# A decoder layer on one core: maxima units in twos between whole blocks, and every block in a PSUM tile of its own

## The chip, the core and the metric

The kernel runs on one core of a Trainium2 chip. Four engines matter here. TensorE (PE) multiplies matrices and writes to PSUM; a second row, PEld, is its weight loading. VectorE (DVE), ScalarE (ACT) and GpSimd (POOL) do the elementwise work, and SyncE (SP) issues most DMAs. Each engine runs its own instructions strictly in the written order and waits at semaphores that the framework sets. The metric is device microseconds (us) of one execution; the median of three runs is 805.79 us (805.64 to 805.87).

## The reference, cut to what matters

A decoder layer in float32: causal self-attention, causal attention of the result over a context, and a feed-forward part with a gated expert, each with its residual; B = 4 batch entries, S = 512 positions, D = 512, 16 heads of 32.

```python
def attention(q, k, v):                      # 4 x 16 heads of 512 x 32
    scores = einsum('bhqd,bhkd->bhqk', q, k) * SCALE
    scores = where(causal, scores, -inf)     # -10000 in the cross-attention
    return einsum('bhqk,bhkd->bhqd', softmax(scores), v)

x = x + attention(x_ln @ wq.T + bq, x_ln @ wk.T + bk, x_ln @ wv.T + bv) @ wo.T + bo
x = x + attention(layernorm(x), ctx, ctx)
f = layernorm(x)
x = x + relu(f @ W_up.T) @ W_down.T + sum_softmax_top2(f @ W_gate.T) * (f @ W_expert)
```

## The kernel before, in words

Everything of one batch entry lies in SBUF. Projections are made in **blocks**: four matmuls of 128x128 weights and 512 columns that add into one PSUM bank (`project`, L229; `project_t`, L241). In float32 each matmul is two records in the trace, so a block is eight records. A head has 32 rows, so the scores of the four heads of a group `g` run side by side in four row groups of the array, as 32x128 matmuls.

An attention goes in two stages. **The maxima** (`with_maxima`, `Attention.maxima`): the row maxima of the scores, to be subtracted before the exponential. There are ten *units* `u0` to `u9`, each one or two pieces `(g, i)` of 512 columns in all, for four heads, in two PSUM tiles `sm` (two heads each; below "a" and "b"). Per unit PE makes the scores (L293), ACT copies each tile to SBUF (L304), POOL masks the diagonal (L312), and DVE takes the maxima (L324). When the last piece of a group is done, `split` cuts the negated maxima into three bfloat16 parts on DVE (L346 to L350), and `rows` turns them over with four PE transposes into a tile `mt` (L361), which DVE, or ACT in the later stage, copies to `mrow` (L367). **The attention itself** (`attend`): ten units again, `S0` to `S9`; `scores` makes the transposed scores (L405) and adds the maxima with a bfloat16 matmul over `mrow` (L416), ACT takes the exponential (L439), POOL masks (L447), and `values` multiplies with v (L482) two units later.

`with_maxima` weaves other blocks between its units, matmul by matmul, as evenly as their number allows: after each unit so many matmuls (`count`) of the blocks in `steps`. What these are differs. In the self-attention of entry 0 they are its own last query and key blocks and its value blocks; of entries 1 and 2 the feed-forward part of the entry before (gate, up, down); of entry 3 four expert blocks and two up blocks. In the cross-attentions they are the query and key blocks of the next entry (and expert blocks in entry 1), in entry 3 the gate and four down blocks. Behind each matmul one `job` is set down: a DVE reduction, the `split`, or a layernorm step of the next entry. A unit's jobs are set down in the gap after the *next* unit.

`ps` is a pool of four PSUM tiles of two banks, each 512 floats wide (`pair`). Blocks come in twos: a query and a key block share a tile, as do two value, up, down or expert blocks, and one instruction of ACT or DVE empties both (value: L685 on DVE; up: L790 on ACT; down: L843 on DVE; query and key are two ACT instructions, L645 and L648, after the second; expert: L867 on DVE, one for each). A new tile takes the one of the four that was released first in the written order. PE then waits until the last reader of the old content is through.

The order of all four engines is the written order (`manual_schedule`).

Of the kernel before, what the change touches and what calls it, by code (L numbers as in the profile page):

```python
# [18 lines left out]
P = 128  # L19
# [7 lines left out]
def decoder_layer(  # L27
# [37 lines left out]
    def pair(name):  # L65

        return ps.tile([P, 2, S], F32, tag="ps", name=name)


# [196 lines left out]
    class Attention:  # L266
# [84 lines left out]

        def rows(self, g, both=None, half=0):


            if both is None:
                tp = ps.tile([P, NT, P], BF16, tag="ps", name=f"mt_{self.name}_{g}")
            else:
                bank = both[:, 0, :].bitcast(BF16)
                tp = bank[:, half * S : (half + 1) * S].rearrange("p (i q) -> p i q", q=P)
            for i in range(NT):  # L360
                nc.tensor.transpose(tp[:, i, :], parts[g % 2][:, i, :], identb)  # L361
            self.mrow[g] = work.tile(
                [P, S], BF16, tag="mrow", name=f"mrow_{self.name}_{g}", bufs=4
            )

            def copy(engine=nc.vector.tensor_copy):
                engine(self.mrow[g], tp.rearrange("p i q -> p (i q)"))  # L367

            return [copy]
# [261 lines left out]
    def query_key(e):  # L631
        b, made = e.b, {}
        e.q_t = act.tile([P, NC, S], F32, tag="q_t", name=f"qT_{b}")
        e.k_t = act.tile([P, NC, S], F32, tag="k_t", name=f"kT_{b}")

        def query(f):
            made[f] = pair(f"pm_qk{b}_{f}")
            yield from project_t(made[f][:, 0, :], wq_sb, e.xn_t, f)

        def key(f):  # L640
            yield from project_t(made[f][:, 1, :], wk_sb, e.xn_t, f)
            out(f)

        def out(f):
            nc.scalar.activation(  # L645
                e.k_t[:, f, :], made[f][:, 1, :], AF.Identity, bias=bk_sb[:, f : f + 1]
            )
            nc.scalar.activation(  # L648
                e.q_t[:, f, :],
                made[f][:, 0, :],  # L650
                AF.Identity,
                bias=bqs_sb[:, f : f + 1],
                scale=SCALE,
            )

        def half(n):

            if n == 0:
                made[0] = pair(f"pm_qk{b}_0")
            rows = slice(n * S // 2, (n + 1) * S // 2)  # L660
            for c in range(NC):
                nc.tensor.matmul(
                    made[0][:, 0, rows],
                    lhsT=wq_sb[:, c, :P],
                    rhs=e.xn_t[:, c, rows],
                    start=(n == 0 and c == 0),
                    stop=(n == 1 and c == NC - 1),
                    skip_group_check=True,
                )

        steps = [(lambda f=f, w=w: w(f)) for f in range(NC) for w in (query, key)]
        if b == 0:
            steps[:1] = [lambda: half(0), lambda: half(1)]
        return steps

    def value(e):
        b, made = e.b, {}
        e.v = act.tile([P, NT, D], F32, tag="v", name=f"v_{b}")

        def one(t):  # L680
            if t % 2 == 0:
                made[0] = pair(f"pm_v{b}_{t}")
            yield from project(made[0][:, t % 2, :], e.xn_t, wv_sb, t)
            if t % 2 == 1:
                nc.vector.tensor_tensor(  # L685
                    e.v[:, t - 1 : t + 1, :],
                    made[0],
                    bv_sb.unsqueeze(1).to_broadcast([P, 2, D]),
                    ALU.add,
                )  # L690

        return [(lambda t=t: one(t)) for t in range(NT)]
# [85 lines left out]
    def ffn(e):  # L778
        b, f_t, made = e.b, e.f_t, {}

        def up(f):
            if f == 0:
                made["h"] = act.tile(
                    [P, NC, S], F32, tag="o_t" if b != B - 2 else "f_t", name=f"hT_{b}"
                )
            if f % 2 == 0:
                made["u"] = pair(f"pm_u{b}_{f}")
            yield from project_t(made["u"][:, f % 2, :], wup_sb, f_t, f)
            if f % 2 == 1:
                nc.scalar.activation(made["h"][:, f - 1 : f + 1, :], made["u"], AF.Relu)  # L790

        def share():

            made["g"] = pair(f"lg_{b}")
            part = made["g"][:, 0, :]
            for c in range(NC):
# [10 lines left out]
        def gate():  # L807
            lg = made["g"][:, 1, : NT * NE].rearrange("p (t e) -> p t e", e=NE)
            for t in range(NT):
# [24 lines left out]
        def down(t):  # L834
            if t % 2 == 0:
                made["d"] = pair(f"pm_d{b}_{t}")
            yield from project(made["d"][:, t % 2, :], made["h"], wdown_sb, t)
            if t == NT - 1 and b == B - 2:
                for n in range(2):
                    aside(f"d{b}_{n}", t - 1 + n, made["d"][:, n, :])  # L840
            elif t % 2 == 1:
                both = e.x[:, t - 1 : t + 1, :]
                nc.vector.tensor_tensor(both, made["d"], both, ALU.add)  # L843

        def expert(t):
            if b == B - 1 and t == NT - 1:
                yield from expert_parts(t)
                return
            last = b == B - 1 and t == NT - 2
            if t % 2 == 0:  # L850
                made["e"] = pair(f"pm_e{b}_{t}")
            yield from project(made["e"][:, t % 2, :], f_t, wexp_sb, t)
            for n in (0,) if last else (0, 1) if t % 2 == 1 else ():
                u = t - t % 2 + n
                weigh(u, made["e"][:, n, :], slice(0, D), nc.sync)

# [47 lines left out]

    def with_maxima(steps, a, first=0, norms=()):


        norms = list(norms)
        run(steps[:first])
        fill = matmuls(steps[first:])  # L910
        total = sum(1 if step.__name__ in ("share", "gate") else NC for step in steps[first:])

        units = []
        for g in range(0, NC, 2):
            units += [[(g, 1), (g + 1, 1)]]
            units += [u for k in (g, g + 1) for u in ([(k, 2), (k, 0)], [(k, NT - 1)])]

        lead = 2 if first else 0
        for _ in range(lead):
            next(fill)  # L920
        done, due, jobs, late = lead, float(lead), [], {3: NC - 1}
        todo = []
        for n, pieces in enumerate(units):
            new = a.maxima(pieces)
            if todo:
                todo.pop()(nc.gpsimd)
            if norms and n % 2 == 0:
                new.append(norms.pop(0))
            due += (total - lead) / len(units)

            count = round(due) - done
            for k in range(count):
                next(fill, None)
                done += 1
                if k == min(1, count - 1) and n in (5, 7):
                    jobs = a.rows((n - 5) // 2) + jobs
                if k == min(1, count - 1) and a.cross and n in (6, 8):
                    todo.append(a.masked(*a.masked_sums((n - 6) // 2)))
                if n == len(units) - 1 and k == count - (2 if count > 4 else 1):
                    if total >= 2 * len(units):  # L940
                        if a.cross:
                            a.rows(2)[0](nc.scalar.copy)
                    else:
                        late = {3: 2, 5: NC - 1}
                run(jobs[:1])
                jobs = jobs[1:]
            run(jobs)
            jobs = new
        for _ in fill:
            pass  # L950
        run(jobs)
        return late

    def attend(a, late):


        units = []
        for g in range(0, NC, 2):
            units += [[(g, 0)], [(g, 3), (g, 1)], [(g, 2), (g + 1, 2)]]
            units += [[(g + 1, 0)], [(g + 1, 3), (g + 1, 1)]]  # L960
        waiting, held, todo = [], [], []

# [12 lines left out]

        for n, pieces in enumerate(units):
            waiting.append(a.scores(pieces))
            if n in late:
# [21 lines left out]
    with tc.manual_schedule(engines=BY_HAND):  # L1000
# [9 lines left out]
        between_self = query_key(e) + value(e)  # L1010
        skip, between_cross, ahead = 5, [], []
        for b in range(B):
            more = b + 1 < B
            sa = Attention(e.q_t, e.k_t, e.v, False, f"s{b}")
            norms, turns = [], []
            if more:
                after, norms, turns = norm_in(b + 1)
            late = with_maxima(between_self, sa, skip, norms)
            if b == B - 1:
                e.x = load_x(b)  # L1020
            attend(sa, late)
            if b > 0:
# [8 lines left out]
            ca.e, ca.out = e, e.beh_t  # L1031
            late = with_maxima(steps[3:], ca)
            if b + 2 < B:
                after.x = load_x(b + 1)
            attend(ca, late)
            if more:
# [75 lines left out]
```

## Time and profile before

| | |
|---|---|
| median of 3 runs | 805.79 us |
| span of the profiled execution (first to last instruction) | 803.7 us |
| busy: PE, DVE, ACT, POOL | 99%, 70%, 49%, 42% of the span |
| mean granted TensorE clock | 0.998 |

The profiled execution's own time is not listed apart; the span is 2.1 us under the median, and that difference is what lies around the span.

The sections of the profiled execution, from the starts of PE's instructions (us; the first row of each pair is from the first maxima unit to the first score matmul):

| | self 0 | cross 0 | self 1 | cross 1 | self 2 | cross 2 | self 3 | cross 3 |
|---|---|---|---|---|---|---|---|---|
| first unit starts | 27.54 | 126.36 | 206.75 | 309.59 | 403.71 | 506.54 | 586.94 | 676.32 |
| maxima last | 39.17 | 30.99 | 43.19 | 44.84 | 43.18 | 30.99 | 33.77 | 29.96 |

In the profile's lines, `pm_v<-wv_sb,xnT 128*128 128x512 f32 x6` reads: six records that write tile pm_v, with 128x128 weights and 512 columns.

### The profile page before, as it was taken

How to read it: one execution, taken by the hardware profiler on the slowest of the kernel's cores; microseconds unless marked ns; L12 is line 12 of the kernel's file. 1: busy time of each engine (PE TensorE's matmuls, PEld its weight loads, DVE VectorE, ACT ScalarE, POOL GpSimd, SP SyncE). 2: the span in 40 equal slices, each digit the busy share in tenths (PEclk: the TensorE clock that was granted, in tenths of full speed). 3: DMA queues.
4: the chain of work that ended last, by engine and by line, in shares of the span. 5: the costliest groups of instructions: out<-in, count | busy, mean ns of one | idle time of the engine just before them, and what ended most of it. 6: DMA issues, size and time to landing. Idle time of an engine off the chain costs nothing.

```text
span 803.7 us, 13927 instructions
## 1 busy us (share of the span) xinstructions
PE 794.0 (99%) x5588; PEld 378.9 (47%) x5592; DVE 565.9 (70%) x963; ACT 395.2 (49%) x448; POOL 339.6 (42%) x523
## 2 busy tenths in 40 slices
PE   8999999999999999999999999999999999999998
PEld 6444454444444454444544455444444444444544
DVE  2378855889679854678867786588959766988512
ACT  2457516871456615567055742687156833674110
POOL 3434612564234732257332482256423652475100
PEclk9999999999999999999999999999999999999999
DMA  9710000001010000021100000000102000000101
GB/s 301 275 28 1 2 1 1 2 27 54 1 27 2 2 0 1 2 78 55 53 14 14 1 2 0 1 1 2 53 28 80 2 1 1 1 2 1 53 1 52
DMA packets 15282, 24.51 MB, mean 30 GB/s; under 512 B 2033, under 2 KB 5361, under 8 KB 15217
## 3 DMA queue, kind: packets, MB, share of 16 engines
q1 hardware_dynamic: 14496, 22.96, 8.6%
q8 instruction: 44, 0.72, 0.4%
q10 hardware_dynamic: 720, 0.66, 0.2%
q14 instruction: 22, 0.17, 0.1%
HBM read 19.42 MB, written 4.19 MB: 29 GB/s over the span
## 4 chain that ended last, share of the span: by engine, by line
PE 95%; ACT 2%; issue 1%; DMA 1%; DVE 0%; ACTq 0%
PE pm_qk L241 14%; PE pm_d L229 7%; PE pm_u L241 7%; PE pm_v L229 7%; PE pm_o L725 7%; PE pm_e L229 7%; PE pv_c L482 6%; PE pv_s L482 6%; PE sm_c L293 6%; PE sm_s L293 6%; PE sc_s L405 5%; PE sc_c L405 5%; PE sc_s L416 1%; PE sc_c L416 1%; PE tp_a L255 1%
## 5 line engine op out<-in xcount | busy, mean ns | idle before, releaser
L324 DVE TENSOR_REDUCE nm_s<-s_s 128x2 f32<-128x1024 f32 (+3 forms) x128 | 96.9, 810 | 34.7 <-POOL s_s L312 34.7
L324 DVE TENSOR_REDUCE nm_c<-s_c 128x2 f32<-128x1024 f32 (+3 forms) x128 | 95.8, 810 | 31.0 <-POOL s_c L312 31.0
L304 ACT COPY s_s<-sm_s 128x1024 f32<-128x1024 f32 x80 | 77.1, 1015 | 70.7 <-PE sm_s L293 36.7
L304 ACT COPY s_c<-sm_c 128x1024 f32<-128x1024 f32 x80 | 77.1, 1016 | 35.9 <-PE sm_c L293 16.2
L312 POOL TENSOR_SCALAR_AFFINE_SELECT s_c<-s_c 128x512 f32<-128x512 f32 (+1 forms) x80 | 43.9, 550 | 100.4 <-ACT s_c L304 100.4
L312 POOL TENSOR_SCALAR_AFFINE_SELECT s_s<-s_s 128x512 f32<-128x512 f32 (+1 forms) x80 | 43.8, 551 | 94.4 <-ACT s_s L304 94.4
L552 DVE TENSOR_TENSOR sum_s<-sum_s,pt_s 128x256 f32<-128x256 f32 (+2 forms) x72 | 59.9, 897 | 15.4 <-PE pv_s L482 15.4
L439 ACT ACTIVATE pt_c<-sc_c 128x1024 f32<-128x1024 f32 x64 | 61.7, 1031 | 18.1 <-PE sc_c L416 10.1
L447 POOL TENSOR_SCALAR_AFFINE_SELECT pt_c<-pt_c 128x512 f32<-128x512 f32 (+1 forms) x64 | 52.9, 833 | 20.7 <-ACT pt_c L439 20.2
L229 PE MATMUL pm_d<-wdown_sb,hT 128*128 128x512 f32 x128 | 61.5, 611 | 0.0
L241 PE MATMUL pm_qk<-xnT,wk_sb 128*128 128x512 f32 x128 | 61.0, 606 | 0.0
L241 PE MATMUL pm_u<-fT,wup_sb 128*128 128x512 f32 x128 | 59.3, 605 | 0.0
L439 ACT ACTIVATE pt_s<-sc_s 128x1024 f32<-128x1024 f32 x56 | 53.9, 1030 | 10.5 <-POOL pt_s L447 5.5
L229 PE MATMUL pm_v<-wv_sb,xnT 128*128 128x512 f32 x128 | 58.8, 600 | 0.0
L725 PE MATMUL pm_o<-wo_sb,oT_s 128*128 128x512 f32 x128 | 57.8, 596 | 0.0
L405 PE MATMUL sc_c<-cqT,ckT 32*128 32x384 f32 (+3 forms) x512 | 56.4, 464 | 0.9 <-ACT sum_c L439 0.9
L241 PE MATMUL pm_qk<-xnT,wq_sb 128*128 128x512 f32 x120 | 56.7, 605 | 0.0
L229 PE MATMUL pm_e<-wexp_sb,fT 128*128 128x512 f32 x120 | 56.3, 604 | 0.0
L447 POOL TENSOR_SCALAR_AFFINE_SELECT pt_s<-pt_s 128x512 f32<-128x512 f32 (+1 forms) x56 | 48.0, 865 | 16.9 <-ACT pt_s L439 16.2
L405 PE MATMUL sc_s<-qT,kT 32*128 32x128 f32 (+3 forms) x512 | 54.1, 464 | 0.9 <-ACT sum_s L439 0.9
L293 PE MATMUL sm_c<-ckT,cqT 32*128 32x512 f32 (+3 forms) x512 | 47.5, 460 | 0.0
L293 PE MATMUL sm_s<-kT,qT 32*128 32x512 f32 (+3 forms) x512 | 47.0, 461 | 0.0
(171 smaller groups left out, 1268.1 us busy)
## 6 DMA issues: line engine op xcount, KB each, us to landing
cv<-in_ctx_dram SPq DMA_DIRECT2D x16, 256.0 KB, 4.4
out_dram<-x SPq DMA_DIRECT2D x15, 256.0 KB, 2.0
xin<-in_x_dram SPq DMA_DIRECT2D x12, 256.0 KB, 2.8
x<-in_x_dram SPq DMA_DIRECT2D x12, 256.0 KB, 4.2
wq_sb<-in_wq_dram SPq DMA_DIRECT2D x2, 512.0 KB, 6.7
wk_sb<-in_wk_dram SPq DMA_DIRECT2D x2, 512.0 KB, 7.7
wv_sb<-in_wv_dram SPq DMA_DIRECT2D x1, 1024.0 KB, 7.8
wo_sb<-in_wo_dram SPq DMA_DIRECT2D x1, 1024.0 KB, 9.5
```

Source lines behind the costliest of these rows:

```text
L229: nc.tensor.matmul(pm, lhsT=lhs_t[:, c, t * P : (t + 1) * P], rhs=w[:, c, :], start=(c == 0), stop=(c == NC - 1),)
L241: nc.tensor.matmul(pm, lhsT=w[:, c, f * P : (f + 1) * P], rhs=rhs_t[:, c, :], start=(c == 0), stop=(c == NC - 1),)
L293: nc.tensor.matmul(scs[r // 2][:, r % 2, c : c + (i + 1) * P], lhsT=self.q_t[h, g, i * P : (i + 1) * P], rhs=self.k_t[h, g, : (i + 1) * P] ...
L304: nc.scalar.copy(s, scs[n])
L312: nc.gpsimd.affine_select(out=diagonal, in_=diagonal, compare_op=ALU.is_ge, fill=NEG, base=0, pattern=[[0, 2], [0, len(pieces)], [-1, P]], ...
L324: nc.vector.tensor_reduce(self.nm[g][:, i, 2 * n : 2 * n + 2], made[n][:, :, c : c + (i + 1) * P], axis=AX.X, op=ALU.max, negate=True,)
L405: nc.tensor.matmul(scs[r // 2][:, r % 2, c : c + S - j * P], lhsT=self.k_t[h, g, j * P : (j + 1) * P], rhs=self.q_t[h, g, j * P :], start= ...
L439: nc.scalar.activation(pt, scs[n], AF.Exp)
L447: nc.gpsimd.affine_select(out=diagonal, in_=diagonal, compare_op=ALU.is_ge, fill=0.0, base=0, pattern=[[0, 2], [0, len(pieces)], [1, P]], ...
L482: nc.tensor.matmul(pv[r * HD : (r + 1) * HD, u, j * P :], lhsT=ones if u else self.v[:, j, h * HD : (h + 1) * HD], rhs=pts[r // 2][:, r % ...
L552: nc.vector.tensor_tensor(to, to, pts[n][:, :, c : c + S - j * P], ALU.add)
L725: nc.tensor.matmul(pms[t // 2][:, t % 2, :], lhsT=a.out[:, c, t * P : (t + 1) * P], rhs=wo_sb[:, c, :], start=(c == 0), stop=(c == NC - 1),)
```

## The change

In words, part by part:

- **Blocks.** Each block (`block`, new) takes a tile of two banks for itself and uses one bank of it; each is emptied by an instruction of its own, half as long a row as before where two were emptied together. The gate's two steps take a tile each.
- **Visits.** `with_maxima` goes through six *visits* in place of ten gaps. Visits 0 to 3 run two units one after the other; visit 4 runs u8 and then S0, visit 5 u9 and then S1. After these comes a given number of whole blocks, `gaps[v]`. So S0 and S1, with their exponentials and masks, stand ahead of the last blocks; `attend` goes on at S2.
- **Jobs.** The jobs of a visit's second unit wait until the next visit, or until a second block of the same visit. They are spread over the four matmuls of a block.
- **Rows.** The transposes of `rows(0)` and `rows(1)` stand after the second matmul of the first block in visits 2 and 3 and write the second bank of that block's tile; the copy to `mrow` is set down first among the jobs that are left. `rows(2)` comes in `attend` (in cross 1 in visit 5, in the block's second bank).
- In self 0 a whole block stands ahead of the first unit, where two matmuls stood.

```diff
+    def block(name):
+        latest["block"] = pair(name)
+        return latest["block"][:, 0, :]
...
         def one(t):
-            if t % 2 == 0:
-                made[0] = pair(f"pm_v{b}_{t}")
-            yield from project(made[0][:, t % 2, :], e.xn_t, wv_sb, t)
-            if t % 2 == 1:
-                nc.vector.tensor_tensor(
-                    e.v[:, t - 1 : t + 1, :],
-                    made[0],
-                    bv_sb.unsqueeze(1).to_broadcast([P, 2, D]),
-                    ALU.add,
-                )
+            pm = block(f"pm_v{b}_{t}")
+            yield from project(pm, e.xn_t, wv_sb, t)
+            nc.vector.tensor_tensor(e.v[:, t, :], pm, bv_sb, ALU.add)
...
-    def with_maxima(steps, a, first=0, norms=()):
+    def with_maxima(steps, a, gaps, first=0, lead=0, norms=()):
...
+        own = [[(0, 0)], [(0, 3), (0, 1)]]
+        visits = [units[0:2], units[2:4], units[4:6], units[6:8], [units[8], None], [units[9], None]]
...
+        for v, two in enumerate(visits):
+            made = [a.maxima(u) if u else [] for u in two]
+            if two[1] is None:
+                begun.append(a.scores(own[len(begun)]))
+            while todo:
+                todo.pop(0)(nc.gpsimd)
+            jobs = pending + made[0]
+            if norms:
+                jobs.append(norms.pop(0))
+            pending = made[1]
+            for n, small, step in blocks(gaps[v]):
+                run(small)
+                if n == 1:
+                    jobs, pending = jobs + pending, []
+                fill = matmuls([step])
+                for k in range(NC):
+                    next(fill)
+                    if n == 0 and k == 1:
+                        if v in (2, 3):
+                            jobs = a.rows(v - 2, latest["block"], bank=1) + jobs
+                        if a.cross and v in (3, 4):
+                            todo.append(a.masked(*a.masked_sums(v - 3)))
+                        if a.cross and v == 5:
+                            a.rows(2, latest["block"], bank=1)[0](nc.scalar.copy)
+                    share = -(-len(jobs) // (NC - k))
+                    run(jobs[:share])
+                    jobs = jobs[share:]
+                for _ in fill:
+                    pass
             run(jobs)
-            jobs = new
...
+        return begun, {3: NC - 1} if 2 in a.mrow else {3: 2, 5: NC - 1}
...
+        gaps_self = [[2, 1, 1, 1, 1, 1], [2, 2, 1, 1, 1, 1], [2, 2, 1, 1, 1, 1], [1] * 6]
+        gaps_cross = [[1, 1, 1, 1, 1, 0], [2, 2, 2, 1, 1, 1], [1, 1, 1, 1, 1, 0], [0, 1, 1, 1, 1, 0]]
```

The query, key, up, down and expert blocks change as `one` of the value blocks does: a tile for each, and an instruction of ACT (query, key, up) or DVE (down, expert) after each.

## The prediction

> **What bounds the kernel now.** First the page's busy shares and its chain of waits: PE is busy for 794.0 of 803.7 us, and 95% of the chain that ends last is PE. So the time changes only by what PE's stream gains, loses or waits for.
>
> ```profile
> PE 794.0 (99%) x5588; PEld 378.9 (47%) x5592; DVE 565.9 (70%) x963; ACT 395.2 (49%) x448; POOL 339.6 (42%) x523
> PE 95%; ACT 2%; issue 1%; DMA 1%; DVE 0%; ACTq 0%
> ```
>
> Then the list of what each engine waited for (engine, line, awaited; us in total, times, longest). PE hardly ever waits with nothing running:
>
> ```profile
> PE sc_s L405 <- ACT sum_s L439: 0.9, 4, 0.2
> PE sc_c L405 <- ACT sum_c L439: 0.9, 4, 0.2
> ```
>
> But a "busy" PE hides two losses, which PE's timeline of self 0 shows (start, us, what):
>
> ```profile
> 35.23 1.14 PE L293 MATMUL sm_s<-kT,qT 32*128 32x512 f32 x8
> 36.30 2.84 PE L241 MATMUL pm_qk<-xnT,wq_sb 128*128 128x512 f32 x6
> 39.08 1.15 PE L293 MATMUL sm_s<-kT,qT 32*128 32x384 f32 x16
> ...
> 66.70 1.14 PE L405 MATMUL sc_s<-qT,kT 32*128 32x512 f32 x8
> ...
> 67.88 1.35 PE L405 MATMUL sc_s<-qT,kT 32*128 32x128 f32 x16
> ...
> 69.16 0.70 PE L405 MATMUL sc_s<-qT,kT 32*128 32x256 f32 x4
> 70.07 0.92 PE L405 MATMUL sc_s<-qT,kT 32*128 32x256 f32 x10 [0.21 <-ACT sum_s L439]
> ...
> 71.35 1.07 PE L482 MATMUL pv_s<-sum_s,v 128*32 128x512 f32 x8
> ```
>
> A block lasts 3.43 us when it runs alone (22.29 to 25.72), 0.4285 a record. From 35.23 to 39.08 PE makes one unit (two streams of 0.43 in four row groups, 0.86) and six records (2.57): 3.43 of work in 3.85. So a round trip from blocks to a unit and back costs **0.42**. And S2 takes 69.16 to 71.35 = 2.19, where S0 takes 1.18 (66.70 to 67.88); 1.28 was expected with its extra pieces, so **0.91** is waiting for S0's exponentials to free PSUM, only 0.21 of it marked.
>
> Last the other engines in the same stage (window; length; busy PE, PEld, DVE, ACT, POOL) and DVE's timeline:
>
> ```profile
> 27.50:66.70 39.20, 39.20 (x197) 16.45 (x197) 28.94 (x54) 21.63 (x24) 14.43 (x28) 1.00 0.25 83
> ...
> 45.68 1.22 DVE L324 TENSOR_REDUCE nm_s<-s_s 128x2 f32<-128x1024 f32 x1 [0.76 <-POOL s_s L312]
> 50.23 0.42 DVE L367 COPY mrow_s<-mt_s 128x512 bf16<-128x512 bf16 x1 [3.32 <-PE mt_s L361]
> ...
> 57.12 1.22 DVE L685 TENSOR_TENSOR v<-pm_v,bv_sb 128x1024 f32<-128x1024 f32 x1 [0.81 <-PE pm_v L229]
> 58.26 0.94 DVE L324 TENSOR_REDUCE nm_s<-s_s 128x2 f32<-128x768 f32 x1
> 59.12 0.41 DVE L367 COPY mrow_s<-mt_s 128x512 bf16<-128x512 bf16 x1
> ```
>
> DVE is 74% busy here but in order: it sits idle 3.32 us for `mt` and later runs behind; its last `split` of self 0 ends near 73.8, seven us after the scores began. Today nobody on PE waits for that.
>
> **The change, part by part.** T is the start of a visit's first unit.
>
> *(a) Round trips removed.* Ten become six in five attentions (4 fewer each), five in cross 0 and 2, whose last visit has no block (5), and four in cross 3 (6). 4×5 + 5×2 + 6 = 36 by 0.42 = **−15.1**. Bounds: 0 if the switch is paid inside a visit too, −15.1.
>
> *(b) S2's wait.* Where a block stands behind S1 (self 0 to 3, cross 1) the exponentials are done before S2: 5 × 0.91 = **−4.6**; bound 0.
>
> *(c) Tiles in a ring.* A visit of two units and one block takes five tiles, of four. So the block behind two units needs the tile of the visit's own first piece, which ACT must have copied. The rows of unit 27.54: PE's streams, then ACT's copy from 28.71 (T+1.17), 1.02 long: PE may start the block at T+2.19 plus about 0.05 = T+2.245. Without the wait it starts after 2 × 0.86 and half of the round trip, T+1.91. Loss 0.335 for each of 28 such visits in the seven attentions other than cross 3: **+9.4**. Bounds 0 (copy started after the first stream) and 28 × 0.9 (a whole copy more).
>
> *(d) `rows` in a block's bank.* The transposes write the second bank of the block's tile, and the written program has the block's third matmul wait for the copy to `mrow` (tile and reader are one name). The copy starts 0.43 after the transposes (49.80 to 50.23), lasts 0.42, and 0.05 passes to PE. The transposes begin at about T+4.07, so the third matmul starts at T+4.97 instead of T+4.3: 0.7 at least, by 16 (two in each attention): **+11.2**. Bounds 0 (the wait does not hold) and the DVE queue: with one reduction of 1.22 ahead, 1.9 each. Behind PE's third matmul stand all of PE's later work, and so ACT's next copies.
>
> A rule of the Trainium skill, PSUM — Partial Sum Buffer, "PSUM bank collisions raise a hardware error", speaks against a wait here: two engines may not touch the same bank in the same 32-partition quadrant, but different banks run clean. By it alone the copy, in the other bank, need not hold the matmuls, and the sum would be less by the 11.2; no run here shows that yet.
>
> *(e) DVE's lateness reaches PE.* With five tiles to a visit in a ring of four, some piece of nearly every later visit needs the tile of an earlier visit's block: in self 0 the second unit of visit 3, S0 in visit 4, S1 in visit 5. Value, down and expert blocks are emptied by DVE (0.68 each, by the 512-column ACT and DVE rows), in the queue behind reductions. DVE's work in a visit is four reductions (the reduce rows: 2.3 to 2.4 a unit, 4.7), a norm step 1.25, the emptying 0.68 = 6.6, with a row copy 7.05, with a `split` (0.95) 7.6. PE's visit is 2 × 0.86 + 0.42 + 3.43 + 0.335 = 5.9. So DVE falls behind by 0.7 to 1.7 a visit, and its position decides. I walked each attention instruction by instruction through the rings and queues. Self 0: the emptying of visit 0's block comes at T+2.15 of visit 3 (needed at 0.97), of visit 1's at T+1.34 of visit 4, of visit 2's at T+2.65 of visit 5, and the row copy of visit 3 at T+5.98. The visits last 9.30, 5.87, 6.88, 8.36, 6.13, 7.66 = 44.2. Without the lateness, but with (a), (c) and (d), they would last 40.8: +3.4. Self 1 and 2 come to 49.5 against 45.65 now, the same +3.4 each (there the gate's exponential stands behind four ACT copies too, and DVE's row copy behind it). Self 3 has ACT emptying most blocks: +0.1. Cross 1 +1.5; cross 3, whose first visit has no block so that four units follow each other at ACT's 1.93 a unit, +1.5. Sum **+13.2**. Bounds: 0, and 6 visits × 4 attentions × 1.45 (7.35 against 5.9) = 35, less the 5.6 of (d) in it = 29; the low part of it, since DVE may also end 6 to 7 us late at no price, as now.
>
> *(f) One more turn-over in `attend`.* `rows(2)` stands there alone in most attentions: from 73.79 to the next values at 74.65 with eight transposes is 0.86, 0.32 of it what four pairs stream by themselves; about 0.31 × 4 (self) + 0.26 × 2 (cross 0, 2) = **+1.7**; bounds 0 and 8 × 0.86.
>
> *At nothing:* two halves in place of one emptying cost DVE 2 × 0.68 against 1.22 and ACT 2 × 0.68 against 1.02; outside the maxima that lies behind PE's 3.43 a block, and inside it is in (e). If that cover went, a block would end 0.14 later. The whole block ahead of self 0's first unit only moves two matmuls (1.71).
>
> Sum: −15.1 − 4.6 + 9.4 + 11.2 + 13.2 + 1.7 = **+15.8**. The profiled span is 803.7; with it 819.5, and with the 2.1 around it 821.6, which against the median of 805.8 is the same 15.8. I say 821.
>
> **The rivals.**
>
> *Faster.* DVE never holds PE: the copy to `mrow` and the emptying are through when PE asks, because the jobs set down in a block are already done. Then (d) and (e) fall: −15.1 − 4.6 + 9.4 + 1.7 = −8.6, **797**. For it: DVE is idle 3.32 us at 50.23 and 26% of the stage. Against it: at 58.26 a reduction stands ahead of the copy already, and the change adds an emptying per block while PE's visit gets shorter. It decides as soon as the row copy's wait on PE's side is under some 0.1 and blocks' emptyings come before T+0.97 of the visit that takes their tile.
>
> *Least waits.* Row copies at 0.7, but no lateness: 16 × 0.7 + 9.4 + 1.7 − 19.7 = +2.6, **808.4**. For it: DVE can start free in each attention. Against it: 6.6 to 7.6 of work in 5.9.
>
> *Worse.* The lateness also reaches S0's and S1's exponentials and masks, so (b) is not had and S2 waits as before: +20.4, **826**. For it: ACT has four copies a visit ahead of the exponentials. Against it: a whole block of 3.43 stands behind S1.
>
> *It does not do what it says:* the round trip is paid between two units of a visit too (their tiles or pieces force it). Then (a) is near 0 and the time 836. Against it: S0 to S1 follow at 1.18, the unit's own streams.
>
> **How the numbers follow.** Forecast 0.77; faster rival 0.10; least waits 0.06; worse 0.06; no removal 0.01. A measurement of this kernel can tell about 0.2% (1.6 us) from no change. Least waits lies at +2.6, so about half of it falls within: faster 0.10, same 0.04, slower 0.86. The range leaves out the faster rival and the ends above: 808 to 829; the upper end is the forecast with (e) at half way to its bound.
>
> **What the profile after would show.** (a) In a visit, two units 0.86 apart, then six or eight block records without a unit among them; PE's busy time in the maxima stages falls while marked waits rise. (b) S2 at 1.2 to 1.3 in self 0. (c) The block's first record about 2.25 after the visit's first unit, released by ACT's copy. (d) A PE wait on DVE's copy from `mt` in the middle of a block, 16 times, 0.7 each or more. (e) PE waits for DVE's instructions on `v`, `x` in visits 3 to 5; the visits of self 0 as listed; self 1 and 2 near 49.5. What would make it wrong: no PE waits on DVE (then 797), or DVE's order such that the emptying comes before the reductions.

## The result and the profile after

The changed kernel takes 834.27 us (median of 4 runs, 833.68 to 834.39) against 805.83 for the kernel before in the same session: a ratio of 1.0359 (95% interval 1.0344 to 1.0373), slower by 28.4 us. The forecast was slower by 15.8, 821 us, with 829 as the upper end. The sign was right and so was the mechanism in the maxima stages, but for the size in cross 3; the attention behind S2 was not, and neither was the size.

The page of the changed kernel, busy shares and the chain of waits that ends last:

```profile
PE 794.5 (95%) x5592; PEld 382.6 (46%) x5592; DVE 576.0 (69%) x978; ACT 396.7 (48%) x456; POOL 330.1 (40%) x523
PE 73%; DVE 14%; ACT 6%; issue 4%; POOL 2%; DMA 1%; ACTq 0%; POOLq 0%; DVEq 0%
```

PE's busy time is the same to 0.5 us (794.0 before), the span is 832.6 instead of 803.7. So all of the loss is PE not running or running slowly, and a quarter of the chain has left PE. What PE waited for (engine, line, awaited; us in total, times, longest):

```profile
PE pm_d L236 <- DVE mrow_s L374: 5.0, 4, 2.0
PE pv_c L565 <- DVE sum_c L559: 4.4, 4, 1.5
PE sc_s L412 <- DVE x L837: 2.7, 2, 1.3
PE pm_k L248 <- DVE mrow_c L374: 1.5, 3, 0.5
...
PE pm_e L236 <- DVE mrow_s L374: 1.5, 2, 1.0
PE pm_v L236 <- DVE mrow_s L374: 1.4, 2, 0.9
PE pm_d L236 <- DVE mrow_c L374: 1.4, 2, 0.9
PE sc_s L412 <- DVE v L689: 1.3, 1, 1.3
...
PE mt_c_both L368 <- DVE behT L600: 1.0, 2, 0.5
```

The rows with `mrow` are the copy in the block's tile (0.6 and 0.3 more stand in two rows left out: 11.7 us on DVE, 16 times). The rows with `x` and `v` are emptied blocks whose tile S1 wants. The second row was not forecast at all: it lies in the cross-attentions, behind S2. PE's timeline of self 0 (start, us, what, and in brackets the idle time before it and who ended it):

```profile
45.25 1.99 PE L236 MATMUL pm_v<-wv_sb,xnT 128*128 128x512 f32 x4 [0.28 <-ACT s_s L311]
47.07 0.39 PE L368 MATMUL pm_v<-identb,parts 128*128 128x128 bf16 x4
47.97 1.99 PE L236 MATMUL pm_v<-wv_sb,xnT 128*128 128x512 f32 x4 [0.52 <-DVE mrow_s L374]
...
65.26 0.38 PE L412 MATMUL sc_s<-qT,kT 32*128 32x128 f32 x4
66.99 1.14 PE L412 MATMUL sc_s<-qT,kT 32*128 32x128 f32 x12 [1.35 <-DVE v L689]
...
71.91 1.15 PE L412 MATMUL sc_s<-qT,kT 32*128 32x256 f32 x16
72.88 0.40 PE L423 MATMUL sc_s<-mrow_s,onesb 32*128 32x256 bf16 x8
73.20 1.06 PE L489 MATMUL pv_s<-sum_s,v 128*32 128x512 f32 x8
```

All three forecast waits are here: the block that waits for the copy of the visit's first piece, the third matmul that waits for the row copy, S1's second tile that waits for the emptying of a value block. S2 now takes 71.91 to 73.20, 1.29, as the sum had it.

Where the time went, from PE's starts in both profiled executions ("behind S2" is from the first matmul with v to the next matmul that is no part of the attention's scores, values and rows, which is the output projection in the self- and a masked sum in the cross-attentions):

| | forecast | measured |
|---|---|---|
| maxima stages, first unit to first matmul with v (the two matmuls of self 0 counted as before) | +14.1 | +18.9 |
| behind S2: self 0 to 3 | +1.2 | +1.85 |
| behind S2: cross 0, 1, 2, 3 | +0.5 | +3.63, -0.25, +3.69, +2.30 |
| before the first unit | 0 | -1.5 |
| the rest | 0 | +0.3 |
| sum | +15.8 | +28.9 |

### The profile page after: what moved, and what is told of

The parts are those of the page before. It is cut to its first block, busy times and chain, and to the rows that moved or that the text cites. A ratio compares the mean times of both kernels' runs of the same rounds, so it can differ in the third digit from the quotient of the medians.

```text
span 832.6 us, 13961 instructions
## 1 busy us (share of the span) xinstructions
PE 794.5 (95%) x5592; PEld 382.6 (46%) x5592; DVE 576.0 (69%) x978; ACT 396.7 (48%) x456; POOL 330.1 (40%) x523
## 4 chain that ended last, share of the span: by engine, by line
PE 73%; DVE 14%; ACT 6%; issue 4%; POOL 2%; DMA 1%; ACTq 0%; POOLq 0%; DVEq 0%
PE pm_u L248 7%; PE pm_o L724 7%; PE pm_q L248 6%; PE pm_k L248 6%; PE pv_c L489 5%; PE pm_e L236 5%; PE pv_s L489 5%; PE sc_s L412 5%; PE pm_d L236 5%; DVE nm_s L331 4%; PE pm_v L236 4%; PE sm_c L300 3%; PE sc_c L412 3%; PE sm_s L300 2%; ACT s_s L311 2%
## 5 line engine op out<-in xcount | busy, mean ns | idle before, releaser
L446 ACT ACTIVATE pt_s<-sc_s 128x1024 f32<-128x1024 f32 x56 | 54.3, 1022 | 26.4 <-issue 11.2
L248 PE MATMUL pm_k<-xnT,wk_sb 128*128 128x512 f32 x128 | 59.8, 604 | 3.3 <-DVE mrow_c L374 1.5
L454 POOL TENSOR_SCALAR_AFFINE_SELECT pt_s<-pt_s 128x512 f32<-128x512 f32 (+1 forms) x56 | 43.9, 792 | 38.9 <-ACT pt_s L446 38.6
L248 PE MATMUL pm_u<-fT,wup_sb 128*128 128x512 f32 x128 | 57.2, 599 | 0.6 <-ACT s_s L311 0.6
L248 PE MATMUL pm_q<-xnT,wq_sb 128*128 128x512 f32 x120 | 54.9, 598 | 1.8 <-ACT s_c L311 1.2
L412 PE MATMUL sc_c<-cqT,ckT 32*128 32x128 f32 (+3 forms) x512 | 54.6, 458 | 1.3 <-ACT s_c L311 0.6
L300 PE MATMUL sm_c<-ckT,cqT 32*128 32x512 f32 (+3 forms) x512 | 45.1, 453 | 0.9 <-ACT s_c L311 0.7
L559 DVE TENSOR_TENSOR sum_c<-sum_c,pt_c 128x256 f32<-128x256 f32 (+2 forms) x48 | 44.8, 998 | 0.9 <-PE pv_c L489 0.9
```

What stands on the lines that cost most here:

```text
L248: nc.tensor.matmul(pm, lhsT=w[:, c, f * P : (f + 1) * P], rhs=rhs_t[:, c, :], start=(c == 0), stop=(c == NC - 1),)
L300: nc.tensor.matmul(scs[r // 2][:, r % 2, c : c + (i + 1) * P], lhsT=self.q_t[h, g, i * P : (i + 1) * P], rhs=self.k_t[h, g, : (i + 1) * P] ...
L412: nc.tensor.matmul(scs[r // 2][:, r % 2, c : c + S - j * P], lhsT=self.k_t[h, g, j * P : (j + 1) * P], rhs=self.q_t[h, g, j * P :], start= ...
L446: nc.scalar.activation(pt, scs[n], AF.Exp)
L454: nc.gpsimd.affine_select(out=diagonal, in_=diagonal, compare_op=ALU.is_ge, fill=0.0, base=0, pattern=[[0, 2], [0, len(pieces)], [1, P]], ...
L559: nc.vector.tensor_tensor(to, to, pts[n][:, :, c : c + S - j * P], ALU.add)
```

## The experiments

Eleven kernels ran, one of them twice, each beside runs of the kernel before; the ratios are to those (medians 803.8 to 804.2), so they compare with 1.0359 for the changed kernel.

**Rows behind the fourth matmul.**

```diff
-                    if n == 0 and k == 1:
+                    if n == 0 and k == NC - 1:
                         if v in (2, 3):
                             jobs = a.rows(v - 2, latest["block"], bank=1) + jobs
```

> The transposes of `rows` stand behind the fourth matmul of their block instead of the second, so no matmul of that block follows the copy to `mrow`. Theory A (the copy holds PE, and the time comes back when nothing stands behind it): PE's marked waits for the copy, 12.4 us in the changed kernel, are gone; in self 0 to 2 a part comes back as a later emptying, so the time falls by 7 to 12, to 822 to 827, and the clock dip behind the 2.0 us wait in self 1 goes with it. Theory B (in self 0 to 2 DVE's own amount of work sets the pace, wherever the wait stands): only the cross-attentions and self 3 gain, about 5, to 829 to 831.

Measured: 839.91 us, ratio 1.0451 (1.0431 to 1.0470), slower than the changed kernel. The waits for the copy were gone, and another stood in their place. PE's waits in this kernel, and below them a line of its timeline of self 0:

```profile
PE pm_d L368 <- DVE x L837: 8.9, 5, 2.8
PE pm_e L368 <- DVE x L857: 5.4, 4, 2.8
```

```profile
58.94 0.38 PE L368 MATMUL pm_v<-identb,parts 128*128 128x128 bf16 x4 [1.65 <-DVE v L689]
```

A generator's emptying is written as its fourth matmul is drawn, so the transposes now stand behind it in the written order, and they wait for DVE to empty *the other bank* of the tile. Both theories miss. What the run shows is the rule behind (d): the order is kept by tile and not by bank, so whatever shares a tile is queued behind the tile's readers, also those of the other bank.

**ACT empties value and down blocks.**

```diff
-            nc.vector.tensor_tensor(e.v[:, t, :], pm, bv_sb, ALU.add)
+            nc.scalar.copy(e.v[:, t, :], pm)
+            nc.gpsimd.tensor_tensor(e.v[:, t, :], e.v[:, t, :], bv_sb, ALU.add)
...
-                nc.vector.tensor_tensor(xt, pm, xt, ALU.add)
+                some = work.tile([P, D], F32, tag="some", name=f"some_d{b}_{t}", bufs=1)
+                nc.scalar.copy(some, pm)
+                nc.gpsimd.tensor_tensor(xt, xt, some, ALU.add)
```

> Value and down blocks are emptied by an ACT copy and finished by a POOL addition, so DVE has no part in giving back their tiles. Theory A (DVE's lateness reaches PE through the emptying): PE's waits for DVE on v and x (4.2 us marked) are gone and the later row copies come up to 0.7 sooner: 3 to 8 less, 826 to 831. Theory B (the ring of four tiles alone holds PE; who empties does not matter, ACT stands behind four copies instead): no less than 833, or more.

Measured: 826.25, ratio 1.0278 (1.0253 to 1.0303): 0.0081, 6.5 us off, as theory A had it. Self 0 falls by 2.07. In it the wait for `v` at S1 is gone, but the row copy of visit 3 now holds PE for 1.69 where it held it for 0.89 (PE's timeline of this kernel): one wait had hidden a part of the next.

```profile
55.71 1.98 PE L236 MATMUL pm_v<-wv_sb,xnT 128*128 128x512 f32 x4 [1.69 <-DVE mrow_s L374]
```

**The split of the last group set down later.**

```diff
+            if v == 5 and not gaps[v]:
+                a.pending = jobs[-1:]
+                jobs = jobs[:-1]
             run(jobs)
...
+                if waiting[0][0][1] == 2:
+                    run(getattr(a, "pending", []))
+                    a.pending = []
```

> In cross 0, 2 and 3, where no block stands behind the last unit, DVE's `split` of the last group is set down behind the first additions of the sums in the attention itself. Theory A (what cross 0, 2 and 3 lose behind S2, 3.6, 3.7 and 2.3 us, is DVE late with those sums): 5 to 8 less, 826 to 829, and the waits of PE for the sums, 4.4 us marked, nearly gone. Theory B (it is the extra turn-over of `rows` and the masked sums, or ACT): 833 to 835 as before the edit.

Measured: 840.49, ratio 1.0455 (1.0436 to 1.0474): both theories miss. The additions started 1.17 us after the first matmul with v, exactly as in the kernel before, and yet the six took 6.96 where they had taken 5.04 (DVE's timelines of this kernel and, below it, of the one before):

```profile
165.67 6.96 DVE L559 TENSOR_TENSOR sum_c<-sum_c,pt_c 128x256 f32<-128x256 f32 x6 [0.54 <-PE pv_c L489]
```

```profile
163.31 5.04 DVE L552 TENSOR_TENSOR sum_c<-sum_c,pt_c 128x256 f32<-128x256 f32 x6 [0.56 <-PE pv_c L482]
```

The split, pushed behind them, then delayed what DVE does next: the transposes of `mt_c_both` waited 6.9 us in three places for DVE's reading of a PSUM tile (`behT`), and cross 0 took 21.09 behind S2. So an earlier start did not help the additions; something slowed them. POOL's timeline, in which S2's masks come late, led to the experiment on `masked` below.

**All three edits.**

> The three edits together (rows behind the fourth matmul, ACT empties value and down blocks, the late split). Theory A (three causes in different places): the gains add, 15 to 24 less, 810 to 819, still above the kernel before because the wait for the first copied tile (0.335 in each visit) stays and eats what the pairs save. Theory B (one cause, DVE's amount of work, seen in three places): the gains overlap, not below 822.

Measured: 833.39, ratio 1.0361 (1.0346 to 1.0377). The time lies where theory B had it (not below 822), but two of the three edits only move a wait, so this tells little of its reason: self 0 to 2 gain (42.3, 48.6, 48.6), the cross-attentions lose what these two cost them.

**POOL's multiplications first.** POOL's timelines around S2 of cross 0, of the kernel before and of the changed one (the first matmul with v starts at 162.14 and 165.00):

```profile
157.90 1.27 POOL L388 TENSOR_TENSOR behT<-ct_c,behT 128x512 f32<-128x512 f32 x1
159.25 1.27 POOL L389 TENSOR_TENSOR ct_c<-ct_c,cnt 128x512 f32<-128x512 f32 x1
...
163.62 0.64 POOL L447 TENSOR_SCALAR_AFFINE_SELECT pt_c<-pt_c 128x512 f32<-128x512 f32 x1 [0.28 <-ACT pt_c L439]
```

```profile
165.58 0.64 POOL L454 TENSOR_SCALAR_AFFINE_SELECT pt_c<-pt_c 128x512 f32<-128x512 f32 x1 [0.28 <-ACT pt_c L446]
166.16 0.10 POOL L394 MEMSET ct_c<- 128x1 f32 x1
166.34 1.27 POOL L395 TENSOR_TENSOR behT<-ct_c,behT 128x512 f32<-128x512 f32 x1
167.69 1.31 POOL L396 TENSOR_TENSOR ct_c<-ct_c,cnt 128x512 f32<-128x512 f32 x1
168.95 5.94 POOL L454 TENSOR_SCALAR_AFFINE_SELECT pt_c<-pt_c 128x512 f32<-128x512 f32 x6
```

Before, the multiplications of `masked` (L388, L389) were over before S0's masks. In the changed kernel they are popped behind S1's masks and stand ahead of S2's, whose masks come 3.95 after the first matmul with v instead of 1.48.

```diff
+            while todo:
+                todo.pop(0)(nc.gpsimd)
             made = [a.maxima(u) if u else [] for u in two]
             if two[1] is None:
                 begun.append(a.scores(own[len(begun)]))
-            while todo:
-                todo.pop(0)(nc.gpsimd)
```

> In a visit of the cross-attention POOL's two multiplications of `masked` are set down ahead of the visit's unit instead of behind S1's masks. Theory A (cross 0, 2 and 3 lose behind S2 because those multiplications, 1.27 and 1.31 us, stand on POOL between S1's masks and S2's, with no block to cover them, and slow DVE's small steps and additions while they run): S2's masks come 2 to 2.6 sooner, and cross 0, 2 and 3 together get back 5 to 8 us: ratio to before 1.025 to 1.030, where the changed kernel had 1.0359. Theory B (DVE is late there with its own work, the reductions and the split): less than 1.5 us in all, ratio 1.034 or more.

Measured: 828.52, ratio 1.0297 (1.0278 to 1.0316). Behind S2, cross 0, 2 and 3 take 16.90, 16.90 and 17.58 instead of 19.16, 19.22 and 19.40: **6.4 us** back at the place named. The time as a whole fell by less (0.0062, 5.0 us), because in this execution self 2 lost 1.4 to a lower clock (below). Theory A holds: where the multiplications stand in POOL's queue was the cause. Theory A names two ways for it to act, the late masks and DVE's slower steps and additions beside the multiplications; both went with the edit, and no run separates them.

**Rows in a tile of their own.**

```diff
-                            jobs = a.rows(v - 2, latest["block"], bank=1) + jobs
+                            jobs = a.rows(v - 2) + jobs
```

> The transposes of `rows` in visits 2 and 3 go to a PSUM tile of their own instead of the second bank of the block's tile. Theory A (the block is held because the tile that it shares with the copy is one to the framework): PE's 12.4 us of waits for the copy are gone; a sixth tile in these visits moves the ring by one, so the next visit needs the emptied block 0.86 after its start and not later, which gives back 0 to 8 in self 0 to 2 and cross 1: 4 to 12 less, ratio 1.021 to 1.031. Theory B (DVE's amount of work sets the pace of self 0 to 2): only the cross-attentions and self 3 gain, 5, ratio 1.030 or above.

Measured: 829.32, ratio 1.0316 (1.0298 to 1.0334): within theory B's range and just outside theory A's, though the interval reaches into both. No PE wait for DVE's copy is left (ACT's in cross 1, 0.7, was not edited), as theory A had it. The stages of cross 0 and 2 fall by 1.2 each; self 0 stays at 45.42 to the hundredth and self 2 falls by 0.5, as theory B had it. Behind S2, cross 0, 2 and 3 lose 0.4, 0.9 and 1.8 more than in the changed kernel; why was not taken apart. PE's timeline of self 0 in this kernel shows where the gain went:

```profile
51.68 1.13 PE L300 MATMUL sm_s<-kT,qT 32*128 32x512 f32 x4 [0.86 <-DVE v L689]
...
59.07 0.70 PE L412 MATMUL sc_s<-qT,kT 32*128 32x512 f32 x2 [0.42 <-DVE v L689]
...
66.67 1.14 PE L412 MATMUL sc_s<-qT,kT 32*128 32x128 f32 x12 [1.35 <-DVE v L689]
```

In self 0 every wait for the copy has become a wait for DVE's emptying of a value block.

**S0 and S1 ahead, alone, in the kernel before.**

```diff
             if todo:
                 todo.pop()(nc.gpsimd)
+            if n >= 8:
+                begun.append(a.scores(own[n - 8]))
```

> The kernel before with one part of the change alone: S0 set down behind unit u8 and S1 behind u9, blocks woven as they were. Theory A (four tiles bound it: a block in progress holds one, u8 two, so S0's second tile has to wait for ACT's copy of u8's first, 2.24 after the unit's start where 1.39 was needed, 0.85 twice in each of eight attentions; against it S2's wait of 0.91 goes): +6, ratio 1.005 to 1.010. Theory B (S0 and S1 ahead of the last matmuls cost nothing): eight times 0.91 gained, ratio 0.991.

Measured: 823.76, ratio 1.0247 (1.0227 to 1.0268), much worse than theory A. The waits that A named are there (9.0 us marked, for ACT's copies, up to 0.94), but behind them come longer ones, 6.6 us in three places and 1.5 more in cross 1, up to 2.3 each:

```profile
PE mt_s_both L361 <- DVE parts L350: 6.6, 3, 2.3
PE sc_s L405 <- ACT s_s L304: 4.8, 7, 0.9
PE sc_c L405 <- ACT s_c L304: 4.2, 7, 0.9
```

With S0 and S1 done earlier PE reaches the last `rows` sooner, and DVE's last `split` is not ready: the lateness of DVE that cost the kernel before nothing. Of the loss in the profiled execution 11.5 lie up to the first matmul with v, and 7.0 behind it.

**A tile for each block, alone, in the kernel before** (the blocks of the changed kernel, the ten gaps of the old one), run twice.

> The kernel before with the other part alone: each block in a tile of its own, emptied by an instruction of its own, in the old order of ten gaps. Theory A (the tiles by themselves are not what costs; the order of whole blocks is): within 2 us, ratio 0.998 to 1.003. Theory B (an emptying for each block on DVE and a ring that turns faster hold PE in any order): 4 us or more slower, ratio 1.005 or above.

> The kernel before with a tile and an emptying for each block, in the old order of ten gaps, again with more rounds. Theory A (the small gain of the first look, ratio 0.9988, is real: about 0.14 to 0.3 in the stages of self 0 to 2 and cross 0 and 2 each): ratio 0.998 to 0.9995. Theory B (it was noise): an interval that holds 1.

Measured: 803.08, ratio 0.9988 (0.9978 to 0.9997), and 802.94, ratio 0.9980 (0.9971 to 0.9989). The tiles do not cost; they bring 1 to 1.6 us, 0.13 to 0.3 in each stage of self 0 to 2 and cross 0 and 2.

**The three repairs that held.** The edits of ACT's emptying, POOL's order and the rows' own tile together; and, on top, the layernorm steps taken out of the visits:

```diff
-            if norms:
-                jobs.append(norms.pop(0))
...
+            if n in (3, 5, 7, 9) and a.norms:
+                run([a.norms.pop(0)])
```

> The changed kernel with three repairs: ACT empties value and down blocks (POOL adds), POOL's multiplications of `masked` ahead of the visit's unit, the transposes of `rows` in a tile of their own. Theory A (three causes; and what the own tile gave back was DVE's late emptying, which ACT now does): the gains of the three (ratios 1.0278, 1.0297, 1.0316 against 1.0359) add or better: 0.008 + 0.006 + 0.004 off, ratio 1.012 to 1.018; still above the kernel before, since a pair of units saves 5.98 - 5.93 = 0.05 us where 0.42 was hoped for. Theory B (one resource, DVE's time, behind all three): ratio 1.022 or above.

> The kernel of three repairs, and the layernorm steps of the next entry (1.25 us of DVE in each of five visits of self 0 to 2) set down in the attention itself instead. Theory A (what is left in self 0 to 2 is the two units' copies and the ring; DVE's amount of work is not the pace there): within 2 us of the three repairs, or worse if the steps are late for the transposes. Theory B (DVE's amount of work per visit is the pace): 3 to 6 us less in self 0 to 2.

Measured: 805.06, ratio 1.0010 (1.0001 to 1.0020), and 807.14, ratio 1.0034 (1.0022 to 1.0046). The three alone took 6.5, 5.0 and 3.5 us off, 15.0 in all; together they take off 0.0349, **28.1**, better than theory A's range. They more than add, in part since two of them are waits in series. Stage by stage (first unit to first matmul with v, us):

| | before | changed | ACT empties | rows' own tile | all three |
|---|---|---|---|---|---|
| self 0 | 43.82 | 45.42 | 43.35 | 45.42 | 40.70 |
| self 2 | 47.84 | 51.06 | 50.47 | 50.54 | 46.08 |
| cross 0 | 35.79 | 36.35 | 36.35 | 35.16 | 35.17 |
| cross 1 | 49.49 | 51.06 | 51.06 | 49.75 | 49.91 |

The kernel before has 1.71 more in self 0 than the others: two matmuls of a block that those make ahead of the first unit. The 50.47 of self 2 holds a stretch of half clock (439.2 to 442.6); self 1, with the same visits at full clock, takes 49.02 there.

In self 0 the row copy and the emptying stand one behind the other: taking away one brings 2.1 or 0.0, taking away both 4.7. Counted at full clock, self 0 to 2 together get back 7.5 more from both than from each alone. The rest of the 13.1 by which the three together beat their sum was not taken apart; each of the three alone still has one or two stretches of half clock, and the kernel of all three has none. PE's timeline of visit 3 there is free of DVE:

```profile
49.30 2.01 PE L300 MATMUL sm_s<-kT,qT 32*128 32x384 f32 x24
51.59 1.98 PE L236 MATMUL pm_v<-wv_sb,xnT 128*128 128x512 f32 x4 [0.28 <-ACT s_s L311]
53.41 0.39 PE L368 MATMUL mt_s<-identb,parts 128*128 128x128 bf16 x4
53.64 1.94 PE L236 MATMUL pm_v<-wv_sb,xnT 128*128 128x512 f32 x4
55.50 1.15 PE L300 MATMUL sm_s<-kT,qT 32*128 32x384 f32 x16
```

Taking five layernorm steps out of the visits as well leaves the stages of self 0 to 2 at 40.70, 46.08 and 46.08, unchanged to the hundredth. So with the repairs in, DVE's amount of work does not set the pace of these visits: no marked wait of PE in them is for DVE. For the changed kernel this does not follow. There DVE's timeline of self 0 shows no idle stretch from 47.49 to 71.3, while PE waits for its copy and its emptying, and no run took the layernorm steps out of that kernel. (Set down in the attention, the steps cost 0.6 in each of self 0 to 2 between the first matmul with v and the output projection.)

**Each order where it pays.** Visits with the repairs in self 0 to 2, the old order with a tile for each block in self 3 and the cross-attentions, both rows turned over together in `attend` as before:

```diff
+            if b < B - 1:
                 begun, late = with_maxima(
                     between_self, sa, gaps_self[b], skip, 1 if b == 0 else 0, norms
                 )
+            else:
+                begun, late = woven(between_self, sa, skip, norms)
...
-            begun, late = with_maxima(steps[3:], ca, gaps_cross[b])
+            begun, late = woven(steps[3:], ca)
```

> Visits of two units with the three repairs in self 0 to 2 alone, where they made the stage shorter than in the kernel before (by 3.1, 1.8 and 1.8 us); the old order of ten gaps, with a tile for each block, in self 3 and the cross-attentions; `rows(2)` and `rows(3)` turned over together as before. Theory A (visits pay where every block stands on an engine that is early, and the turn-over of 0.45 in each attention comes back): 2.3 + 0.9 + 0.9 from the stages and attentions, 0.45 three times, 0.3 from the cross-attentions' tiles: 4 to 6 us under the kernel before, ratio 0.992 to 0.995. Theory B (with the turn-over together `split` of the last group is late in self 0 to 2 and PE waits for it): ratio 0.996 to 1.000.

Measured: 799.14 us, ratio **0.9945** (0.9931 to 0.9959): faster than both, as theory A had it. Self 0 to 2 take 3.12, 1.82 and 1.82 less up to the first matmul with v, and the part behind it is as before to 0.02. Of the 3.12 in self 0, 1.71 are the two matmuls that only moved ahead of the first unit; 1.4 is the gain.

## Why the prediction was right in sign and wrong in size

*(a) and (c), pairs and the ring: right.* A visit of two units and one block takes 5.93 in cross 0; 5.90 had been worked out. Two gaps with the same work took 2 x 2.99 = 5.98. So of 0.42 for each round trip removed, 0.05 was kept.

*(b) S2: right where a block stands behind S1* (1.29). That S0 and S1 ahead are a gain by themselves is not so: alone they cost 20 us (with one dip of the clock of the kind told of below among them).

*(d) the row copy: right,* 16 waits and 11.7 us for 16 x 0.7 = 11.2. That the sums are so close is in part luck: the single marked waits run from 0.3 to 2.0. The rule of the Trainium skill weighed there (PSUM — Partial Sum Buffer, "PSUM bank collisions raise a hardware error") was no guide to the time: that two banks do not collide is not contradicted by a run here, but the written order waits by tile. The tile of its own, in which no bank is shared, removed the wait; the transposes behind the fourth matmul, in the other bank still, did not.

*(e) DVE's lateness: right in self 0 to 2, too small in cross 3.* Self 0 measured 9.31, 5.87, 6.92, 8.19, 6.22, 7.62 for the forecast 9.30, 5.87, 6.88, 8.36, 6.13, 7.66; self 2 comes to 49.8 for the forecast 49.5. (From 45.65 to 49.5 are, with (a), (c) and (d) taken off, 2.8 for (e) in self 1 and 2 each, and not the 3.4 that went into the sum.) The explanation under it, "DVE falls behind" by its work per visit, fits DVE's timeline of self 0 but was not tried in this kernel. In cross 3, by the forecast's terms, the stage was to grow by 0.4 (-2.5, +1.4 and the +1.5 of (e)). It grew by 4.0 in the changed kernel, and by 3.5 in the POOL repair, whose visits 0 to 3 are the same and which had full clock there: **3.1** more than forecast. PE waits there for DVE to empty the first down block, which the forecast for cross 3 did not name (PE's waits in the POOL repair):

```profile
PE pm_d L236 <- DVE x L837: 0.8, 1, 0.8
```

The two row copies behind it hold PE for 1.8 where 1.4 was forecast. That is 1.2 of the 3.1; the rest was not taken apart. With the three repairs the stage is 2.7 shorter than in the POOL repair.

*The step that failed most is (f)*, with the last clause of (e), "since DVE may also end 6 to 7 us late at no price, as now". The prediction walked the maxima through the queues and took the attention behind S2 as unchanged but for one more turn-over, +1.7. It measured +11.2. Of the 9.5 missed, **6.4** are POOL's two multiplications of `masked`, which the change moves past S1's masks and in front of S2's; moving them back brought 6.4 at that place. It was a step moved in a queue that was not followed: in the prediction POOL's queue does not occur. Cross 1, which has a block behind S1 as cover, lost nothing (-0.25). The other 3.1 lie behind S2 too (over the kernel before and with the forecast's 1.7 in them: 1.37, 1.37 and 0.48 in cross 0, 2 and 3 after the repair, 0.45 to 0.51 in each self-attention); 0.50 in cross 0 and 2 each is a marked wait of the transposes for a PSUM tile that DVE reads, the rest was not taken apart. With the rows turned over together as before, in the last kernel, the part in self 0 to 2 is gone.

*The clock, which the sum did not have: 2.0.* Self 1 has the same visits as self 2 and lost 1.54 more in visits 2 and 3; cross 3 took 12.33 for its first four units and block, where every other kernel with the same order there took 10.64, 1.69 less. In both places the granted clock is down. In cross 3 most of it came back at once, since DVE's emptying was through when the longer block ended and PE did not wait for it: the stage took 38.57, and 38.11 in the POOL repair, so 0.5 is the price there. The windows of self 1 (window; length; busy PE, PEld, DVE, ACT, POOL; granted clock, DMA):

```profile
241.00:241.50 0.50, 0.50 (x3) 0.26 (x2) 0.47 (x2) 0.00 (x0) 0.00 (x0) 1.00 0.00 0
241.50:242.00 0.50, 0.50 (x3) 0.03 (x1) 0.43 (x3) 0.00 (x0) 0.00 (x0) 0.63 0.00 0
242.00:243.00 1.00, 1.00 (x6) 0.11 (x4) 0.38 (x3) 0.00 (x0) 0.00 (x0) 0.50 0.00 0
243.00:244.00 1.00, 1.00 (x8) 0.71 (x12) 1.00 (x2) 0.00 (x0) 0.00 (x0) 0.50 0.00 0
...
245.00:245.50 0.50, 0.50 (x8) 0.10 (x4) 0.50 (x2) 0.43 (x1) 0.42 (x2) 0.95 0.00 0
```

Half clock for some 3.4 us, from 1.2 us after the end of PE's 2.0 us wait for the row copy:

```profile
240.38 2.58 PE L236 MATMUL pm_d<-wdown_sb,hT 128*128 128x512 f32 x4 [2.00 <-DVE mrow_s L374]
```

The same wait in self 2 left the clock alone in this execution, and the clock fell behind it in that of the POOL repair. In cross 3 no wait of PE stands ahead of the dip (705.8 to 709.3); there its four units, 3.4 us of streams, are spread over 6.1.

*What balances:* the other maxima stages, -0.3 together (self 3 has +0.7), and a start 1.5 earlier, which is no merit of the change: the first 16 transposes ran at a granted clock of 0.57 in the profile before and at 1.00 after. Sum: 15.8 + 6.4 + 3.1 (behind S2) + 3.1 (cross 3) + 2.0 - 0.3 - 1.5 + 0.3 = 28.9, the difference of the spans.

*The rivals.* "Faster" fell at the point named: PE does wait for DVE's row copy, 0.3 to 2.0 each time. "Worse" gave 826 by a cause that did not happen (S2 does not wait as before). The low ends were out of reach.

## What to carry to other kernels

Follow every queue that a moved step is moved past, the quiet ones too: what broke the sum was a 2.6 us step on an engine that is 40% busy. When a wait is found, ask which wait ends next behind it: two in series show little when each is taken away alone, and far more than their sum together. Before grouping units to save a switch, count the buffers that the group holds: five tiles in a ring of four gave back 0.37 of every 0.42.

## What was not expected of the hardware

**Small DVE steps slowed by POOL.** A subtraction on 128x16 takes 0.18 in the kernel before, and 1.14 in the changed one while POOL multiplies (166.34 to 169.00):

```profile
166.51 1.14 DVE L355 TENSOR_TENSOR rest_c<-nm_c,parts 128x16 f32<-128x16 f32 x1
167.69 0.20 DVE L356 CAST parts<-rest_c 128x16 bf16<-128x16 f32 x1
167.92 1.16 DVE L357 TENSOR_TENSOR parts<-rest_c,parts 128x16 bf16<-128x16 f32 x1
```

The cast between them, with one input, keeps its 0.20. The Trainium skill (SBUF — State Buffer, "Who interferes with whom") says that a DVE instruction with two SBUF inputs contends with a GpSimd instruction that reads SBUF, and that one with at most one SBUF input, outside the modes that use two ports, does not; these rows agree. A cast is not free of it everywhere, though. In the kernel before one takes 0.67 while POOL masks:

```profile
161.81 0.67 DVE L349 CAST parts<-rest_c 128x16 bf16<-128x16 f32 x1
```

```profile
161.79 0.64 POOL L447 TENSOR_SCALAR_AFFINE_SELECT pt_c<-pt_c 128x512 f32<-128x512 f32 x1 [0.49 <-ACT pt_c L439]
```

**A wait of PE may cost more than itself.** In the profiled executions every dip of the clock after the start lies in a version that has a PE wait of 2.0 us or more somewhere; the kernel before, the three repairs (with the layernorm steps in either place), the one with a tile for each block and the last kernel show none once started. The Trainium skill (TensorE: Matmul & The Clock Gate, "What's actually happening") tells of a free-running window of about 3.4 us after which an idle PE gets half its clock. The 3.4 us at 0.50 agree, and that an equal wait is punished in one execution and not in another fits a window that runs freely. That a whole window has to be idle does not fit: PE's wait ahead of the dip in self 1 is 2.0, and in cross 3 none is marked. What sets the dips off stays open; no run here tried it by itself.
